# All eight experts add into the output, VectorE's order in the relation stage is written out, and loads and copies around it move

## The chip, the cores and the metric

The kernel runs on one core of one Trainium2 chip. The metric is device time in microseconds (us) of one execution, as the median of several; lower is better. The engines are TensorE (PE), VectorE (DVE), ScalarE (ACT), GpSimd (POOL) and SyncE (SP). SP and POOL start most of the DMAs here, ACT a few.

## The reference

Four residual layers on 625 tokens of 1024 numbers, each on the layernorm of `x` (cut to what matters):

```python
# 1 relational graph convolution with a gate (8 relations; edges: src, dst, edge_type)
out = x @ root + bias
for r in range(8):
    sums = segment_sum(x[src] * (edge_type == r), dst)
    cnt = segment_sum(edge_type == r, dst)
    out = out + (sums / max(cnt, 1)) @ weight[r]
z = concat([u, x]) @ w_gate + b_gate          # u is out
h = tanh(u) * z + x * (1 - z)
# 2 int8 feed-forward:  x_int8 @ weight_int8.T, scaled, plus bias
# 3 graph convolution:  segment_sum(norm * (x @ W.T + b)[col], row)
# 4 mixture of 8 experts, top 2, capacity 196 slots per expert
logits = x @ router_w
combine, dispatch = top2_gating(logits, capacity)
expert_in = einsum('nec,nh->ech', dispatch, x)
hmid = silu(einsum('ech,ehf->ecf', expert_in, w1) + b1)
expert_out = einsum('ecf,efh->ech', hmid, w2) + b2
y = einsum('nec,ech->nh', combine, expert_out)
out = y + 0.1 * (silu(x @ sw1 + sb1) @ sw2 + sb2)     # and x + out
```

## The kernel before

Tokens lie in five tiles (`t`) of 125 partitions (P = 125, NT = 5); the 1024 columns are worked in two halves (`h`, HC = 512).

*Products of weights.* Nine products of the normalized tokens with a 1024 x 1024 weight (relations 0 to 6, the gate's x half, relation 7) run on PE by a scheme with seven block products in place of eight (L431, combinations on VectorE). Relations 0 to 6 go to DRAM as `yd`; the rows of relation 7, the last product, stay in SBUF. Meanwhile VectorE and GpSimd count, for each relation, the edges from each token to each token, into the DRAM table `counts`.

*The relation stage* (L571 to L707) goes through the relations in the order 7, 0, 1, ... 6 (`order`; `n` is the place in it). For each relation, half and tile, `products` (L629) multiplies counts with rows `y`: five source tiles, each in two parts, so ten matmuls into one PSUM tile. The two parts are `hi`, a rounded copy that ScalarE makes (L602), and `lo`, the rest, which VectorE gets by subtraction (L606, the split). VectorE then does `X += ps * rc` (L684). `rc` is one over the number of edges: VectorE adds the counts over the five source tiles (`over_sources`, L614 and L616), PE sums them (`number`, L642), VectorE inverts (L648, L649). `over_relations` sums the counts over relations into `btot`, by ScalarE's copy for the first relation (L622) and VectorE's additions for the others (L624). While half 0 of a relation is multiplied, its half 1 is split and the next relation's `over` is summed; during half 1 the next relation's half 0 is split and `btot` is summed. In each tile's step the code writes L684, a split, and a count addition; a planner decides the order in which VectorE executes them from their due times, within the bounds that data and `behind` set.

*Orders.* `behind(a, b)` only says that `a` is issued after `b` on an engine; `after` makes it wait for the end of `b`. `in_order` chains SP's loads in the order of the code: the count tiles (`load_counts`, three buffers `bp`), rows (`load_y`) and weights (`weight_block`). `on_pe` and `in_steps` chain PE's work.

*The gate stage* (L710 to L828) multiplies by `w_gate`, whose four 1 MB blocks `gate_w` are loaded at n = 5. Its normalized tiles `th` are transposed between the gate's tiles, `th[t - 2]` at t = 2 and 3.

*The experts.* The router's masks (L1063 to L1147) give each token its slot in two experts. `fill_slots` (L1159) makes, by small matmuls, for each expert's 196 slots (two groups of 98, index `j`) the token number `token_i` and the gate's weight; an empty slot's token number points to a spare row past the 625. `find_others` and `fill_others` (L1187, L1198) find tokens that are not in an expert, one for each empty slot, so that an empty slot can add zero to some row of `out`: `out_i`. Before the change this is made for experts 4 to 7 (NL = 4) only: VectorE makes 20 one-hot tiles `spots`, PE sums them with 40 matmuls.

`shared_out` (L1227) finishes the tokens' base value in `X` (VectorE's `z` and `X` additions) and stores it. Then, for each expert e, come the gather of its tokens (L1278, GpSimd), transposes, two matmul steps (L1294, L1322), the scaling (L1329, VectorE, into `ye`, two buffers in the memory of `aT` and `btot`) and the addition of the rows to DRAM (L1339, GpSimd's indirect DMA that adds; two per expert, four half as wide for expert 7, with `half_i`). Each addition waits for those of the expert before, because two experts may add to one row.

The base goes into a DRAM tensor `total`, which has spare rows for empty slots. Experts 0 to 3 add to `total` at `token_i`; one copy `out <- total` (L1363, on SP) follows once they have landed; experts 4 to 7 wait for it and add to `out` at `out_i`.

A second, exact version of everything stands under a condition on the counts that does not hold for these inputs.

Of the kernel before, what the change touches and what calls it, by code (L numbers as in the profile page):

```python
# [35 lines left out]
NL = 4  # L36
# [11 lines left out]
def layers(  # L48
# [166 lines left out]
    total = dram.tile([N + 2 * CP, D], F32, name="total")  # L215
# [358 lines left out]
    bp = convs.enter_context(tc.tile_pool(name="bp", bufs=3))  # L574
    hp = convs.enter_context(tc.tile_pool(name="hp", bufs=2 * NT))
    crp = convs.enter_context(tc.tile_pool(name="crp", bufs=2))
# [4 lines left out]
    counted, over, parts = {}, {}, {}  # L581

    def load_counts(r):
        counted[r] = bp.tile([P, NT, N], FR, tag="b", name="b")
        for d in spread(nc.sync, counted[r].bitcast(F32), counts[r].rearrange("(k p) d -> p k d", p=P)):
            after(in_order(d), group)

    def load_y(r, h):
        for k in range(NT):
            y = yp.tile([P, HC], FR, tag="y", name="y")  # L590
            for d in spread(nc.sync, y.bitcast(F32), ydram[r][:, h, k, :]):
                in_order(d)
            held.setdefault(r, {})[k, h] = y

    def split(r, h, k):

        y = held[r][k, h].bitcast(F32)
        if exact:
            parts[r, h, k] = [y]
            return  # L600
        hi = hp.tile([P, HC], F32R, tag="hi", name="hi")
        nc.scalar.copy(hi, y)  # L602
        lo = held[r][k, h]
        if r == order[0]:
            lo = yp.tile([P, HC], F32R, tag="y", name="y")
        nc.vector.tensor_sub(lo, y, hi.bitcast(F32))  # L606
        parts[r, h, k] = [lo, hi]

    def over_sources(r, k):

        v = counted[r].bitcast(F32)
        if k == 1:
            over[r] = crp.tile([P, N], FR, tag="over", name="over")
            d = nc.vector.tensor_add(over[r], v[:, 0, :], v[:, 1, :])  # L614
        else:
            d = nc.vector.tensor_add(over[r], over[r].bitcast(F32), v[:, k, :])  # L616
        behind(d, posted[-1])

    def over_relations(r, k):
        v = counted[r].bitcast(F32)[:, k, :]  # L620
        if r == order[0]:
            behind(nc.scalar.copy(btot[:, k, :], v), copied[-1])  # L622
        else:
            behind(nc.vector.tensor_add(btot[:, k, :], btot[:, k, :], v), posted[-1])  # L624
# [41 lines left out]
    for k in firsts:  # L666
        split(order[0], 0, k)
    for n, r in enumerate(order):
        if n == R - 3:
            gate_w = [[weight_block(w_gate, i, h) for i in range(2)] for h in range(2)]  # L670
        for h in range(2):
            hs = slice(h * HC, (h + 1) * HC)
            for t in range(NT):
                ps = mm_tile()
                on_pe(products, ps, r, h, t, firsts if n == 0 and h == 0 else range(NT))
                if (n, h, t) == (0, 0, 0):
                    on_pe(number, r)
                if h == 1 and t == 0 and n + 1 < R:
                    on_pe(number, order[n + 1])
                if n == R - 1 and h == 1:  # L680
                    on_pe(turn_u, t, 0)
                    if t > 0:
                        on_pe(turn_u, t - 1, 1)
                nc.vector.scalar_tensor_tensor(  # L684
                    X[t][:, hs],
                    ps[:P, :],
                    rc[:, r, t : t + 1],
                    X[t][:, hs],
                    op0=ALU.mult,
                    op1=ALU.add,  # L690
                )
                if h == 0:
                    split(r, 1, t)
                    if t > 0 and n + 1 < R:
                        over_sources(order[n + 1], t)
                else:
                    if n + 1 < R:
                        split(order[n + 1], 0, t)
                    over_relations(r, t)
            if n == 0 and h == 0:  # L700
                load_y(order[1], 0)
                load_y(order[1], 1)
            elif 0 < n + h and n + 1 + h < R:
                load_y(order[n + 1 + h], 1 - h)
        if n + 3 < R:
            load_counts(order[n + 3])
# [68 lines left out]
    for t in range(NT):  # L775
# [4 lines left out]
        for h in range(2):  # L780
            with tc.issue_after(pe_last.ins):
                pe_last, added = gate(t, h)
            if h == 0 and t >= 2 and t < NT - 1:
                on_pe(transposed, xT, (t - 2) * P, th[t - 2], P)
            if t > 0:
                nc.scalar.copy(wb[(t - 1) // 2][:, (t - 1) % 2 * 2 + h, :], w8[:, 2 * (t - 1) + h, :])
# [159 lines left out]
    cleared = []  # L946
    for v in (tokens, total):
        for j in range(2):
            cleared.append(nc.scalar.dma_start(v[N + j * CP : N + (j + 1) * CP, :], zrow))
# [124 lines left out]
    NM = 2 * NE + NL  # L1074
# [19 lines left out]
    nc.vector.tensor_add(others, masks[:, :, 0, NE - NL :], masks[:, :, 1, NE - NL :])  # L1094
# [80 lines left out]
    spots = aT_flat[:, : NL * NT * CAP // 2].bitcast(BF16)  # L1175
    spots = spots.rearrange("p (e t c) -> p e t c", e=NL, t=NT)
    before = mp.tile([P, NT, NL], F32, name="before")
    out_i = mp.tile([CP, 2, NL], I32, name="out_i")
    half_i = mp.tile([CP, 2, 2], I32, name="half_i")

    def find_others():

        nc.vector.tensor_scalar(before, others, -float(N), float(N), op0=ALU.mult, op1=ALU.add)
        nc.vector.tensor_add(before, before, pos_all[:, :NT, 2 * NE :])
        for e in range(NL):
            for t in range(NT):
                d = nc.vector.tensor_scalar(  # L1187
                    spots[:, e, t, :], io_cap, before[:, t, e : e + 1], None, op0=ALU.is_equal
                )
                behind(d, numbered[-1])  # L1190

    def fill_others(_):
        ps = ps_sm.tile([128, HC], F32, tag="sm", name="others")
        ps = ps[:CP, : 4 * NL].rearrange("p (j e v) -> p j e v", j=2, e=NL)
        for j in range(2):
            for e in range(NL):
                for t in range(NT):
                    last = nc.tensor.matmul(  # L1198
                        ps[:, j, e, :],
                        spots[:, e, t, j * CP : (j + 1) * CP],  # L1200
                        digits[:, t, :],
                        start=(t == 0),
                        stop=(t == NT - 1),
                    )
        rest_of = mp.tile([CP, 2, NL], F32, name="rest_of")
        taken_of = slots[:, :, NE - NL :, 0]
        nc.vector.tensor_scalar(rest_of, ps[:, :, :, 0], float(P), None, op0=ALU.mult)
        nc.vector.tensor_add(rest_of, rest_of, ps[:, :, :, 1])
        nc.vector.tensor_scalar(out_i, taken_of, -1.0, 1.0, op0=ALU.mult, op1=ALU.add)
        nc.vector.tensor_mul(rest_of, rest_of, out_i)  # L1210
        nc.vector.tensor_add(out_i, rest_of, slots[:, :, NE - NL :, 1])
        for h in range(2):
            nc.vector.tensor_scalar(
                half_i[:, h, :], out_i[:, :, NL - 1], 2.0, float(h), op0=ALU.mult, op1=ALU.add
            )
        return last
# [3 lines left out]
    base = []  # L1220

    def shared_out(t):
# [16 lines left out]
        base.extend(spread(nc.sync, total[t * P : (t + 1) * P, :], X[t]))  # L1239
# [3 lines left out]
    find_others()  # L1243
    in_steps(((shared_out, 0), (shared_out, 1), (fill_others, None), *((shared_out, t) for t in range(2, NT))))
# [8 lines left out]
    def rows_at(j, e, direct=False):  # L1253
        at = out_i[:, j, e - NE + NL :][:, :1] if direct else token_i[:, j, e : e + 1]
        return bass.IndirectOffsetOnAxis(ap=at, axis=0)

    def flat_rows(v):
        return v[:N, :].rearrange("n d -> (n d)").rearrange("(a b) -> a b", a=80)
# [17 lines left out]
    def gather(e):  # L1276
        for j in range(2):
            nc.gpsimd.indirect_dma_start(  # L1278
                out=rows_of_slots(e, j), out_offset=None, in_=tokens, in_offset=rows_at(j, e)
            )  # L1280
# [25 lines left out]
    done = sent  # L1306
    sent = base + cleared

    def expert_out(e):
# [4 lines left out]
        for j in range(2):  # L1314
# [3 lines left out]
            for h in range(2):  # L1318
# [15 lines left out]
                if e < NE - 1:  # L1334
                    to, at, v = total if e < NE - NL else out, rows_at(j, e, e >= NE - NL), ye[:, j, :]
# [18 lines left out]
    for e in range(NE):  # L1354
# [5 lines left out]
        if e == NE - NL:  # L1360
            for n in range(e + 4, NE):
                load_weights(n)
            d = in_order(nc.sync.dma_start(flat_rows(out), flat_rows(total)))  # L1363
            after(d, [*sent, *done])
            sent = [d]
# [62 lines left out]
```

## Time and profile before

| | us |
|---|---|
| three runs | 1248.88, 1250.09, 1253.97 (median 1250.09) |
| the profiled execution | 1246.61 |
| its span, first to last recorded instruction | 1244.9 |
| PE busy (share of the span) | 1188.5 (95%) |
| VectorE busy | 837.9 (67%) |
| GpSimd busy | 487.0 (39%) |
| ScalarE busy | 172.2 (14%) |
| mean clock granted to TensorE | 0.985 |
| L629, 800 matmuls of the relation stage | 323.5 |
| L606, 80 splits, mean of one | 53.0 relation stage, 0.680 each |
| PE's last matmul (L1322) starts | 1221.69, for 0.59 |

A row of the timeline has the start, the length, the engine, the source line, the operation, output and inputs, and in brackets the idle time before it and what ended that. Equal instructions that follow one another are put together (x5). A row of the windows has the stretch, its length and each engine's busy time and instructions, then the clock granted to TensorE (1.00 is full), the busy share of the DMA engines and GB/s. A row of the waits has what waited, for what, the sum, how often, and the longest.

### The profile page before, as it was taken

How to read it: one execution, taken by the hardware profiler on the slowest of the kernel's cores; microseconds unless marked ns; L12 is line 12 of the kernel's file. 1: busy time of each engine (PE TensorE's matmuls, PEld its weight loads, DVE VectorE, ACT ScalarE, POOL GpSimd, SP SyncE). 2: the span in 40 equal slices, each digit the busy share in tenths (PEclk: the TensorE clock that was granted, in tenths of full speed). 3: DMA queues.
4: the chain of work that ended last, by engine and by line, in shares of the span. 5: the costliest groups of instructions: out<-in, count | busy, mean ns of one | idle time of the engine just before them, and what ended most of it. 6: DMA issues, size and time to landing. Idle time of an engine off the chain costs nothing. (4 is left out here: it accounts for less than half of the span.)

```text
span 1244.9 us, 11083 instructions
## 1 busy us (share of the span) xinstructions
PE 1188.5 (95%) x3810; PEld 649.8 (52%) x3810; DVE 837.9 (67%) x1340; ACT 172.2 (14%) x308; POOL 487.0 (39%) x227
## 2 busy tenths in 40 slices
PE   5999999999999999999999999899999999999992
PEld 2444444444444444444448887685445447756661
DVE  6879888888888888865149778755979416452210
ACT  1100000000000000000022122113321111313330
POOL 1005787888787888888500000004210000043312
PEclk9999999999999999999989999999999999999996
DMA  9995737373636364535455667606430025279964
GB/s 263 267 255 131 200 65 198 66 198 70 194 75 188 81 183 87 146 78 142 76 142 156 168 161 198 216 1 167 118 136 16 17 84 177 79 223 279 278 186 71
DMA packets 156288, 181.72 MB, mean 146 GB/s; under 512 B 78513, under 2 KB 95272, under 8 KB 156160
## 3 DMA queue, kind: packets, MB, share of 16 engines
q1 hardware_dynamic: 66162, 134.84, 36.7%
q0 software_dynamic: 72992, 13.31, 10.5%
q10 hardware_dynamic: 17070, 32.78, 8.6%
q8 instruction: 32, 0.52, 0.2%
q14 instruction: 32, 0.26, 0.1%
HBM read 134.22 MB, written 48.86 MB: 147 GB/s over the span
## 5 line engine op out<-in xcount | busy, mean ns | idle before, releaser
L389 POOL DMA_INDIRECT table<-hits,idx x165 | 403.8, 2447 | 199.4 <-DMA kr<-key_rows 99.7
L431 PE MATMUL mm<-w,xT 128*125 128x512 f32 x800 | 350.9, 593 | 0.0
L365 DVE SCALAR_TENSOR_TENSOR junk<-kr,key,wm 125x1375 f32<-125x1375 f32 x165 | 271.4, 1645 | 1.1
L431 PEld LDWEIGHTS mm<-w,xT 128*125 128x125 f32 x800 | 150.2, 188 | 191.7 <-issue 189.1
L629 PE MATMUL mm<-y,b 125*125 125x512 f32 x400 | 163.0, 407 | 9.1 <-DVE y L606 6.7
L629 PE MATMUL mm<-hi,b 125*125 125x512 f32 x400 | 160.5, 401 | 0.0
L431 PE MATMUL mm<-t,btot 128*125 128x512 f32 x320 | 143.8, 592 | 0.0
L1278 POOL DMA_INDIRECT th<-tokens,token_i x16 | 21.5, 1345 | 205.0 <-DVE aT L1187 172.7
L431 PEld LDWEIGHTS mm<-t,btot 128*125 128x125 f32 x320 | 60.1, 188 | 77.3 <-issue 77.3
L684 DVE SCALAR_TENSOR_TENSOR X<-mm,rc,X 125x512 f32<-125x512 f32 x80 | 59.9, 749 | 51.5 <-PE mm L629 50.4
L952 POOL IOTA io<- 125x40 f32 x1 | 0.2, 208 | 239.3 <-PE mm L629 239.3
L629 PEld LDWEIGHTS mm<-y,b 125*125 125x125 f32 x400 | 75.9, 190 | 32.2 <-DVE y L606 11.1
L629 PEld LDWEIGHTS mm<-hi,b 125*125 125x125 f32 x400 | 76.1, 190 | 18.1
L900 PE MATMUL mm<-w,xT 128*125 128x512 f32 x160 | 70.0, 595 | 2.4 <-ACT xT L187 2.4
L431 PE MATMUL mm<-w,btot 128*125 128x512 f32 x160 | 71.9, 592 | 0.0
L431 PE MATMUL mm<-t,xT 128*125 128x512 f32 x160 | 71.9, 592 | 0.0
L746 PE MATMUL mm<-w,xT 128*125 128x512 f32 x160 | 69.3, 592 | 0.0
L602 ACT CAST hi<-y 125x512 fp32r<-125x512 f32 x80 | 43.3, 617 | 147.2 <-PE mm L629 132.4
L1322 PE MATMUL mm<-w,th 128*98 128x512 f32 x128 | 56.3, 592 | 0.0
L606 DVE TENSOR_TENSOR y<-y,hi 125x512 fp32r<-125x512 f32 x80 | 53.0, 680 | 0.7 <-ACT hi L602 0.7
L450 ACT COPY y<-mm 125x512 f32<-125x512 f32 x18 | 10.5, 586 | 302.0 <-PE mm L431 291.7
L900 PEld LDWEIGHTS mm<-w,xT 128*125 128x125 f32 x160 | 29.6, 188 | 39.7 <-issue 36.0
(219 smaller groups left out, 1165.4 us busy)
## 6 DMA issues: line engine op xcount, KB each, us to landing
w<-in_L_gnn_weight_dram SPq DMA_DIRECT2D x32, 1024.0 KB
w<-in_L_ffn_w_dram SPq DMA_DIRECT2D x16, 1024.0 KB
yd<-y ACTq DMA_DIRECT2D x70, 224.0 KB
y<-yd SPq DMA_DIRECT2D x70, 224.0 KB
table<-zero SPq DMA_DIRECT2D x4, 3054.0 KB
b<-table SPq DMA_DIRECT2D x8, 1367.2 KB
kr<-key_rows ACTq DMA_DIRECT2D x15, 601.6 KB
w<-in_L_gnn_w_gate_dram SPq DMA_DIRECT2D x8, 1024.0 KB
```

The source lines that it names most:

```text
L365: d = nc.vector.scalar_tensor_tensor(junk, kr, key[:, c : c + 1], wm[:, (EG - 1 - j) * P : (2 * EG - 1 - j) * P], op0=ALU.is_equal, op1=AL ...
L389: d = nc.gpsimd.indirect_dma_start(out=table, out_offset=bass.IndirectOffsetOnAxis(ap=idx[:, c : c + 1], axis=0), in_=hits[:, c : c + 1], ...
L431: last = nc.tensor.matmul(ps[:P, :], lhs[:, k], rhs[:, k], start=(start and k == 0), stop=(stop and k == 3))
L450: nc.scalar.copy(put(NT - 1, h), ps[:P, :])
L602: nc.scalar.copy(hi, y)
L606: nc.vector.tensor_sub(lo, y, hi.bitcast(F32))
L629: last = nc.tensor.matmul(ps[:P, :], counted[r][:, k, t * P : (t + 1) * P], part, start=(k == ks[0] and part is parts[r, h, k][0]), stop=( ...
L684: nc.vector.scalar_tensor_tensor(X[t][:, hs], ps[:P, :], rc[:, r, t : t + 1], X[t][:, hs], op0=ALU.mult, op1=ALU.add,)
L746: last = nc.tensor.matmul(ps[:P, :], xT[:, 4 * i + k, t * P : (t + 1) * P], gate_w[h][i][:, k, :], start=(i == 0 and k == 0), stop=(i == 1 ...
L900: last = nc.tensor.matmul(ps[:P, :], xT[:, k, t * P : (t + 1) * P], gcn_w[h][k // 4][:, k % 4, :], start=(k == 0), stop=(k == KD - 1),)
L1278: nc.gpsimd.indirect_dma_start(out=rows_of_slots(e, j), out_offset=None, in_=tokens, in_offset=rows_at(j, e))
L1322: last = nc.tensor.matmul(ps[:CP, :], he[:, f, j * CP : (j + 1) * CP], weights[e][1][:, f, hs], start=(f == 0), stop=(f == 1),)
```

## The change

- `NL` and `total` go. `tokens` alone is cleared in its spare rows; the base is stored to `out`; the copy L1363 goes; all eight experts add into `out` at `out_i`.
- The masks of "others" cover eight experts: 40 one-hots in place of 20, ten after each of the first four `shared_out`, and 80 matmuls in `fill_others`, which comes after the fifth `shared_out` instead of the second.
- In the relation stage `in_turns` and `turns` chain VectorE's accumulations, splits and count additions in one order. In half 0: accumulation 0, splits 0 and 1; accumulation 1, split 2, `over` 1; accumulation 2, split 3, `over` 2; and so on. In half 1 likewise, with `btot` 0 to 4. The first half is special: its first accumulation comes after tile 1, with three splits there.
- The first relation's `over` additions go behind `posted[-3]` in place of `posted[-1]` (`posted` lists VectorE's additions of the weight products); the first split is issued ahead of them. `number` of that relation follows tile 1 in place of tile 0.
- ScalarE's `hi` copies go behind its last copy in the units (`copied[-1]`), and the `btot` copies behind the last upper half's copy.
- Count tiles have named memory `b0`, `b1`, `b2`; the third lies in memory of its own pool `bp2`. The first rows of the second relation have tiles of their own (`yp2`) and are loaded before the loop.
- The four blocks of `w_gate` are loaded one per half at n = 3 and 4, in place of all four at n = 5.
- In the gate stage `th[t - 3]` is transposed at t = 3 and 4.

```diff
-    total = dram.tile([N + 2 * CP, D], F32, name="total")
...
-    bp = convs.enter_context(tc.tile_pool(name="bp", bufs=3))
+    bp = convs.enter_context(tc.tile_pool(name="bp", bufs=1))
+    bp0, bp1 = (bp.tile([P, NT, N], FR, tag=f"b{i}", name=f"b{i}") for i in range(2))
     hp = convs.enter_context(tc.tile_pool(name="hp", bufs=2 * NT))
+    bp2 = convs.enter_context(tc.tile_pool(name="bp2", bufs=1))
+    yp2 = convs.enter_context(tc.tile_pool(name="yp2", bufs=NT))
...
-        nc.scalar.copy(hi, y)
+        upper.append(nc.scalar.copy(hi, y))
+        behind(upper[-1], copied[-1])
...
-        nc.vector.tensor_sub(lo, y, hi.bitcast(F32))
+        turns.append(nc.vector.tensor_sub(lo, y, hi.bitcast(F32)))
+        if len(turns) > NT:
+            behind(*turns[:-3:-1])
...
+    def in_turns(d):
+        if turns:
+            behind(d, turns[-1])
+        turns.append(d)
...
-        behind(d, posted[-1])
+        if r == order[0]:
+            behind(d, posted[-3])
+        else:
+            in_turns(d)
...
-            behind(nc.scalar.copy(btot[:, k, :], v), copied[-1])
+            d = nc.scalar.copy(btot[:, k, :], v)
+            if not exact:
+                behind(d, upper[2 * NT - 1])
         else:
-            behind(nc.vector.tensor_add(btot[:, k, :], btot[:, k, :], v), posted[-1])
+            in_turns(nc.vector.tensor_add(btot[:, k, :], btot[:, k, :], v))
...
+    load_y(order[1], 0)
+    gate_w = [[], []]
     for n, r in enumerate(order):
-        if n == R - 3:
-            gate_w = [[weight_block(w_gate, i, h) for i in range(2)] for h in range(2)]
         for h in range(2):
+            if n in (3, 4):
+                gate_w[n - 3].append(weight_block(w_gate, h, n - 3))
...
-                if (n, h, t) == (0, 0, 0):
+                if (n, h, t) == (0, 0, 1):
                     on_pe(number, r)
...
+                for k in ((0, 1), (2,), (3,), (4,), ())[t] if n + h > 0 else ((), (0, 1, 2), (3,), (4,), ())[t]:
+                    if h == 0:
+                        split(r, 1, k)
+                    elif n + 1 < R:
+                        split(order[n + 1], 0, k)
+                for k in ((), (1,), (2,), (3,), (4,))[t] if h == 0 else ((), (0,), (1,), (2,), (3, 4))[t]:
+                    if h == 1:
+                        over_relations(r, k)
+                    elif n + 1 < R:
+                        over_sources(order[n + 1], k)
...
-            if h == 0 and t >= 2 and t < NT - 1:
-                on_pe(transposed, xT, (t - 2) * P, th[t - 2], P)
+            if h == 0 and t >= 3:
+                on_pe(transposed, xT, (t - 3) * P, th[t - 3], P)
...
-    NM = 2 * NE + NL
+    NM = 3 * NE
...
-        base.extend(spread(nc.sync, total[t * P : (t + 1) * P, :], X[t]))
+        for d in spread(nc.sync, out[t * P : (t + 1) * P, :], X[t]):
+            after(d, done)
+            base.append(d)
...
-    find_others()
-    in_steps(((shared_out, 0), (shared_out, 1), (fill_others, None), *((shared_out, t) for t in range(2, NT))))
+    for t in range(NT):
+        in_steps(((shared_out, t),))
+        for e in range(2 * t, min(2 * t + 2, NE)):
+            find_others(e)
+    in_steps(((fill_others, None),))
...
-                    to, at, v = total if e < NE - NL else out, rows_at(j, e, e >= NE - NL), ye[:, j, :]
+                    to, at, v = out, rows_at(j, e, out_i), ye[:, j, :]
...
-        if e == NE - NL:
-            for n in range(e + 4, NE):
-                load_weights(n)
-            d = in_order(nc.sync.dma_start(flat_rows(out), flat_rows(total)))
-            after(d, [*sent, *done])
-            sent = [d]
```

## The prediction

> **What bounds the kernel now.** I read the shares of busy time first, then the waits of TensorE (PE), then the timeline around the longest of them, then windows for the granted clock, then the timeline of GpSimd (POOL) at the end.
>
> ```profile
> PE 1188.5 (95%) x3810; PEld 649.8 (52%) x3810; DVE 837.9 (67%) x1340; ACT 172.2 (14%) x308; POOL 487.0 (39%) x227
> PE tr L184 <- DVE X L169: 10.1, 1, 10.1
> PE mm L629 <- DVE y L606: 6.7, 4, 4.3
> ```
>
> PE works 1188.5 of 1244.9 us, so a change pays only where PE waits, where its clock falls, or after its last matmul. The first wait, 10.1 us, is the layernorm at the start, which nothing here touches. The second lies in the relation stage; this is its longest piece:
>
> ```profile
> 804.88 0.80 DVE L616 TENSOR_TENSOR over<-over,b 125x625 fp32r<-125x625 f32 x1
> 805.60 2.24 DVE L624 TENSOR_TENSOR btot<-btot,b 125x625 f32<-125x625 f32 x3
> 807.76 3.09 DVE L606 TENSOR_TENSOR y<-y,hi 125x512 fp32r<-125x512 f32 x5
> 808.49 0.50 PE L629 MATMUL mm<-y,b 125*125 125x512 f32 x1 [4.32 <-DVE y L606]
> 808.00:810.00 2.00, 1.51 (x4) 1.09 (x5) 2.00 (x4) 0.00 (x0) 0.00 (x0) 0.72 0.00 0
> 810.00:812.00 2.00, 2.00 (x6) 1.50 (x6) 0.84 (x2) 0.00 (x0) 0.00 (x0) 0.50 0.00 0
> ```
>
> VectorE (DVE) did four count additions (L616, L624) while PE stood idle for the split of the first row (L606). In the two windows the next-to-last three columns are clock, DMA share and GB/s: the clock then fell to 0.50. So a stall costs twice. The whole price comes from the spacing of the accumulations (L684), one per tile: 8.49 us across this stall where a full-speed tile takes 2.32, so 6.17 lost; from 773.24 to 787.92, with the stalls of 1.25 and 0.59, 14.68 against 4 x 2.32 + 2.88 = 12.16, so 2.52 lost. From 654.38 to 822.54 all of them take 168.16 against 67 x 2.32 + 7 x 0.5 = 158.9: no other loss there exceeds 0.6.
>
> PE's last matmul ends at 1222.29, and 22.6 us follow in which only additions into the output land:
>
> ```profile
> 1180.69 3.23 SPq L1363 DMA_DIRECT2D out_dram<-total  x1
> 1199.63 1.55 POOL L1339 DMA_INDIRECT out_dram<-aT,out_i  x1 [23.13 <-SPq L1384]
> 1211.42 1.52 POOL L1339 DMA_INDIRECT out_dram<-btot,out_i  x1 [0.30 <-issue]
> 1218.86 1.53 POOL L1339 DMA_INDIRECT out_dram<-aT,out_i  x1 [5.92 <-DMA out_dram<-btot,out_i]
> 1220.69 1.52 POOL L1339 DMA_INDIRECT out_dram<-aT,out_i  x1 [0.30 <-issue]
> 1229.24 1.53 POOL L1339 DMA_INDIRECT out_dram<-btot,half_i  x1 [7.03 <-DMA out_dram<-aT,out_i]
> 1234.72 1.52 POOL L1339 DMA_INDIRECT out_dram<-btot,half_i  x1 [0.30 <-issue]
> ```
>
> The 2.5 MB copy holds expert 4's additions until 1199.63, though VectorE had its rows at 1182.75. Experts 5 to 7 queue behind, each pair waiting for the pair before to land (1211.42 to 1218.86 is 7.44, 1220.69 to 1229.24 is 8.55).
>
> **The change, part by part.** *The end.* Without the copy, expert 4's pair starts near 1181 and expert 5's near 1195; both have landed when expert 6 needs them. Expert 6's second half-rows: VectorE's last two L1329 would fall at 1208.5 and 1210.1 as now (PE itself had no wait there). GpSimd sometimes waited for the third L1329 (expert 3: start 1167.46, third one done 1167.02), so the pair starts 1209.6 and 1211.4. It lands at 1218.9 to 1220.0 by the two durations above. Expert 7's four follow every 1.83: last start 1218.9 + 0.2 + 5.5 = 1224.6 (VectorE's last rows, 1223.08, are no bound). From the last start to the end the trace has 1244.9 - 1234.72 = 10.18. End 1234.8 to 1235.9: gain 9.0 to 10.1; I take 9.9, nearer the pair that ran with as little beside it. Upper bound of a landing: expert 0 to 1, 1126.75 to 1138.56, 11.8 while weights load; then the gain is 5.7. Lower: none faster than 7.44 is seen.
>
> An estimate stands apart here: the Trainium skill ("DMA: Bandwidth & Descriptors", "Anatomy of one DMA — SWDGE (gpsimd) path") gives 2.0 us plus bytes over 436 GB/s for GpSimd's DMA, so 2.9 us for 401 KB; by it expert 7's last addition would follow its rows (1223.08 + 0.3) and the end come at 1233.6. The measured 7.44 decides.
>
> *More one-hots and `others` matmuls.* L1187 makes 40 instead of 20, ten behind each of four `shared_out`; 20 x 0.235 = 4.7 us more of VectorE, spread under the 19.4 us that the 40 matmuls of L1227 take. The last one-hot ends about 1110.0 and PE's last `shared_out` about 1107.3; the order on PE is now five `shared_out`, then L1198, then expert 0's transposes. L1198 had 40 matmuls in 1.96 us, so 80 take 3.92: +1.96, and about 0.1 at the join, +2.1. If VectorE's order let the last tile's one-hots come later, PE would wait up to 10 x 0.235 = 2.4. The clock: L1159's small matmuls were followed by this,
>
> ```profile
> 1088.00:1089.00 1.00, 1.00 (x7) 0.76 (x7) 0.54 (x5) 0.47 (x2) 0.00 (x0) 0.88 1.05 371
> 1090.00:1091.00 1.00, 1.00 (x2) 0.34 (x1) 1.00 (x5) 0.00 (x0) 1.00 (x1) 0.50 1.03 416
> 1092.00:1093.00 1.00, 1.00 (x3) 0.38 (x2) 1.00 (x6) 0.00 (x0) 1.00 (x1) 0.91 0.27 94
> ```
>
> so 3.57 us of tiny matmuls cost 0.12 + 3 x 0.5 + 0.09 = 1.7, while the 1.96 us of L1198 were followed by 1.00 throughout. 3.92 us of L1198 and then 1.8 us of transposes resemble the first: I take +1.6, bounds 0 and 3.4 (twice as long a drop).
>
> The skill speaks against this edit: "TensorE: Matmul & The Clock Gate" ("Part 1: The HAM clock gate", "Part 4: PE-mode transpose") says that an idle-looking window of about 3.4 us throttles the array and that transposes do not count as activity. The drop after L1159 agrees. By the rule alone a second drop is near sure, and the sum below stands; by L1198's own row it would be 1.6 lower.
>
> The base goes straight into `out` in the same six stores; two queue behind a weight load on SP's queue, and expert 0's pair waits for them: it started at 1123.31 behind a weight load already, and could be some 3 us later (two issues of 1.3 each, as the six take 7.62) with 14.06 us of PE per expert to recover in, so 0. `b2` of expert 7 waits for the later L1198, is needed at 1211 and hides under six experts. `tokens` alone is cleared: two fewer stores, off the path.
>
> *Fixed VectorE order.* In each later half the first two splits come right behind the first accumulation and the count additions behind the splits. Work is the same: per half five accumulations at 0.67 apart (804.21 to 804.88), five splits at 0.62 (3.09 for five) and four or five additions at 0.72 (2.16 for three): 9.3 to 10.1, against 11.6 of PE. So the 6.17 and 2.52 go: -8.7. Bounds: 0 if the slack of 1.5 us is spent elsewhere, -9.2 by the full sum. The copies of the upper halves (L602) go behind ScalarE's last copy: five take 2.70 a half and ScalarE is busy 14%, so 0; late next would be the split behind each.
>
> *The start.* VectorE's first act at 639.21 is an `over` (0.72 back to back) ahead of the split that L629 needs:
>
> ```profile
> 639.21 0.80 DVE L614 TENSOR_TENSOR over<-b 125x625 fp32r<-125x625 f32 x1
> 639.93 0.68 DVE L606 TENSOR_TENSOR y<-y,hi 125x512 fp32r<-125x512 f32 x1
> 640.71 0.47 PE L629 MATMUL mm<-y,b 125*125 125x512 f32 x1 [2.15 <-issue]
> 642.00:646.00 4.00, 3.79 (x7) 2.11 (x8) 4.00 (x7) 0.00 (x0) 0.00 (x0) 0.50 0.64 185
> ```
>
> That addition now stands behind. PE begins up to 0.7 earlier; -0.5, bounds +0.8 (the first accumulation now comes a tile later and holds a bank) and -3.7, the half-speed stretch 642 to 651.8 shortened if PE starts without the gap. `number` moves one tile, same work. Relation two's rows have own tiles and load from about 636 instead of 640.64, behind the third count load, which now waits for a unit buffer; needed after 654, hidden unless more than 10 us late. One transposition in the gate stage moves a tile later: no PE wait stood there and the count is equal, 0; late next would be FFN operands, bound 0.6.
>
> *w_gate.* Its four 1 MB loads leave the place where they stood together (766 to 773) and go one by one into the halves of the fourth and fifth relation (n = 3, 4), behind each half's rows on SP: 2 x 1.28 MB of rows, 1.5 of counts and 2 of gate per 23.7 us, some 250 GB/s. Windows 770 to 790 moved 300 and 323 GB/s. Rows are asked for a half ahead, so 0; the slow rival prices the other case.
>
> Sum: -9.9 + 2.1 + 1.6 - 8.7 - 0.5 = -15.4. Profiled 1246.61 (span 1244.9 and 1.7 around it) becomes 1231.2; the median of 1250.09 lies 3.5 above the profiled one, so 1234.7.
>
> **Rivals.** (a) *The relation stalls only move.* For: slack is 1.5 us a half, and a split needs ScalarE's copy, then VectorE. Against: both stalls stood behind count additions, never behind copies. The -8.7 falls away: 1243.4. (b) *The end gains little.* If pairs into `out` land in 11.8, the end gains 5.7 instead of 9.9: 1238.9; if something else holds the last pair as long, 1244.6. For: eight experts now add where four did, and the first ran at 11.8. Against: nothing loads after 1185. (c) *Slower: the gate's loads starve the rows.* If the rate while they load falls under 250 GB/s so that rows come over half a relation late, each of four halves stalls like 808 did: 4 x 6.17 = +24.7, 1234.7 + 24.7 = 1259.4. For: DMA share was 1.05 when they loaded before. Against: 300 GB/s was reached then. (d) *The clock never drops at the start:* -3.7 for -0.5, 1231.5.
>
> **Chances.** Forecast 0.68, (a) 0.11, (b) 0.08, (c) 0.05, (d) 0.08. Half a per cent, 6.25 us, is what a measurement can tell: faster 0.92, same 0.04, slower 0.04 (c with little of it). Range: 1228, where (d) meets the best landing and no second drop, to 1243, where (a) ends.
>
> **What would show it.** Right: no L629 wait over 0.5 us between 654 and 822, accumulations of that stretch within 160 us; expert 4's pair within 4 us of its rows; last matmul to end about 12 to 13 us instead of 22.6; half-clock windows behind the `others`. Wrong: a wait on `y` by DMA at n = 3 or 4, or GpSimd still waiting over 5 us ahead of expert 6.

## The result and the profile after

The changed kernel takes 1231.49 us (median of four, 1228.55 to 1232.26) against 1250.05 of the kernel before: a ratio of 0.9842, 95% interval 0.9815 to 0.9869. The forecast was 1234.7, the range 1228 to 1243. Its profiled execution took 1231.8 with a span of 1230.0, 14.9 less than the span before.

The page of the kernel after, its first part, and the rows of PE's waits that answer to those shown before:

```profile
PE 1192.4 (97%) x3850; PEld 653.6 (53%) x3850; DVE 846.7 (69%) x1360; ACT 172.2 (14%) x308; POOL 487.2 (40%) x227
```

```profile
PE tr L183 <- DVE X L168: 10.0, 1, 10.0
...
PE mm L649 <- issue: 1.4, 1, 1.4
...
PE mm L649 <- DVE y L614: 0.6, 1, 0.6
```

The 6.7 us of waits for a split have shrunk to one of 0.6 at the start of the relation stage (L629 is L649 now, the split L614, the accumulation L712). PE is 4 us busier: it has 40 more small matmuls (1.9 us) and more time at half clock. Where the time went, by PE's milestones in the two profiled executions:

| milestone | before | after | difference | change since the line above |
|---|---|---|---|---|
| end of the weight products | 638.57 | 638.54 | 0.0 | |
| last accumulation of the relation stage starts | 848.71 | 838.60 | -10.1 | -10.1 |
| last gate matmul starts | 922.16 | 913.75 | -8.4 | +1.7 |
| last int8 matmul starts | 981.55 | 974.65 | -6.9 | +1.5 |
| last `slots` matmul starts | 1088.18 | 1081.19 | -7.0 | -0.1 |
| first expert's first matmul starts | 1111.3 | 1106.2 | -5.1 | +1.9 |
| last matmul starts | 1221.7 | 1217.8 | -3.9 | +1.2 |
| end | 1244.9 | 1230.0 | -14.9 | -11.0 |

In the relation stage VectorE now works like this (timeline of the kernel after, VectorE, same place as the stall shown before):

```profile
802.54 0.75 DVE L712 SCALAR_TENSOR_TENSOR X<-mm,rc,X 125x512 f32<-125x512 f32 x1 [0.83 <-PE mm L649]
803.21 0.15 DVE L668 TENSOR_SCALAR reached<-tr 125x5 f32<-125x5 f32 x1
803.28 0.68 DVE L614 TENSOR_TENSOR y<-y,hi 125x512 fp32r<-125x512 f32 x1
...
805.43 0.75 DVE L712 SCALAR_TENSOR_TENSOR X<-mm,rc,X 125x512 f32<-125x512 f32 x1 [0.69 <-PE mm L649]
806.10 0.68 DVE L614 TENSOR_TENSOR y<-y,hi 125x512 fp32r<-125x512 f32 x1
806.69 0.81 DVE L644 TENSOR_TENSOR btot<-btot,b 125x625 f32<-125x625 f32 x1
807.75 0.75 DVE L712 SCALAR_TENSOR_TENSOR X<-mm,rc,X 125x512 f32<-125x512 f32 x1 [0.25 <-PE mm L649]
```

Each accumulation is followed by a split and only then by one count addition, and VectorE waits for PE, no longer PE for VectorE. At the end, GpSimd's additions of the kernel after (start, length, operation, idle time before and what ended it):

```profile
1176.48 1.55 POOL L1374 DMA_INDIRECT out_dram<-aT,out_i  x1 [3.87 <-DMA out_dram<-btot,out_i]
1179.16 1.54 POOL L1374 DMA_INDIRECT out_dram<-aT,out_i  x1 [1.14 <-DVE aT L1364]
1189.79 1.52 POOL L1374 DMA_INDIRECT out_dram<-btot,out_i  x1 [9.08 <-DVE btot L1364]
1193.22 1.52 POOL L1374 DMA_INDIRECT out_dram<-btot,out_i  x1 [1.91 <-DVE btot L1364]
1203.85 1.52 POOL L1374 DMA_INDIRECT out_dram<-aT,out_i  x1 [9.11 <-DVE aT L1364]
1207.28 1.52 POOL L1374 DMA_INDIRECT out_dram<-aT,out_i  x1 [1.91 <-DVE aT L1364]
1214.33 1.52 POOL L1374 DMA_INDIRECT out_dram<-btot,half_i  x1 [5.54 <-DVE btot L1364]
...
1219.81 1.52 POOL L1374 DMA_INDIRECT out_dram<-btot,half_i  x1 [0.30 <-issue]
```

From expert 5 on no addition waits for another to land: they wait for their own rows from VectorE, and the last three follow the one before. The last one starts 10.15 before the end, as it did before (10.16), but 1.4 after PE's last matmul ends instead of 12.4. What is new is half clock in other places (windows of the kernel after; the column before the last two is the granted clock):

```profile
842.00:846.00 4.00, 4.00 (x8) 1.67 (x7) 0.00 (x0) 4.00 (x5) 0.37 (x2) 0.57 0.98 256
921.00:928.00 7.00, 6.30 (x24) 4.88 (x25) 5.66 (x15) 2.64 (x6) 0.00 (x0) 0.51 0.01 2
1081.00:1085.00 4.00, 4.00 (x11) 1.89 (x10) 1.95 (x12) 1.30 (x2) 2.09 (x2) 0.57 1.05 394
1105.00:1109.00 4.00, 4.00 (x17) 3.77 (x18) 1.07 (x7) 1.29 (x3) 1.97 (x2) 0.57 1.01 308
```

The third had its like before (1088 to 1093) and the fourth was forecast. The first two are where the table's +1.7 and +1.5 arise; the second lies among transpositions with waits, so that 3.41 by the clock cost PE only 1.5.

### The profile page after: what moved, and what is told of

The parts are those of the page before. It is cut to its first block, busy times and chain, and to the rows that moved or that the text cites. A ratio compares the mean times of both kernels' runs of the same rounds, so it can differ in the third digit from the quotient of the medians.

```text
span 1230.0 us, 11161 instructions
## 1 busy us (share of the span) xinstructions
PE 1192.4 (97%) x3850; PEld 653.6 (53%) x3850; DVE 846.7 (69%) x1360; ACT 172.2 (14%) x308; POOL 487.2 (40%) x227
## 4 chain that ended last, share of the span: by engine, by line
PE 91%; DMA 4%; ACT 2%; DVE 1%; issue 1%; POOL 0%; SPq 0%; ACTq 0%; POOLq 0%; DVEq 0%
PE mm L429 48%; PE mm L649 14%; PE mm L777 6%; PE mm L931 6%; PE mm L1357 4%; PE mm L1330 3%; PE mm L959 2%; DMA w<-in_L_gnn_weight_dram 2%; PE tr L183 2%; PE mm L1259 2%; PE mm L908 1%; PE mm L1045 1%; DMA y<-yd 1%; PE lgT L1032 1%; ACT xT L186 1%
## 5 line engine op out<-in xcount | busy, mean ns | idle before, releaser
L387 POOL DMA_INDIRECT table<-hits,idx x165 | 408.1, 2474 | 198.7 <-DVE idx L383 99.3
L429 PEld LDWEIGHTS mm<-w,xT 128*125 128x125 f32 x800 | 150.1, 188 | 192.3 <-issue 188.6
L649 PE MATMUL mm<-y,b 125*125 125x512 f32 x400 | 160.7, 402 | 2.3 <-issue 1.4
L649 PE MATMUL mm<-hi,b 125*125 125x512 f32 x400 | 159.1, 398 | 0.0
L1314 POOL DMA_INDIRECT th<-tokens,token_i x16 | 17.4, 1086 | 214.5 <-DVE token_i L1198 174.4
L649 PEld LDWEIGHTS mm<-y,b 125*125 125x125 f32 x400 | 75.0, 187 | 23.6 <-DVE y L614 3.4
L712 DVE SCALAR_TENSOR_TENSOR X<-mm,rc,X 125x512 f32<-125x512 f32 x80 | 60.0, 751 | 38.8 <-PE mm L649 38.0
L649 PEld LDWEIGHTS mm<-hi,b 125*125 125x125 f32 x400 | 75.1, 188 | 18.2
L614 DVE TENSOR_TENSOR y<-y,hi 125x512 fp32r<-125x512 f32 x80 | 53.6, 681 | 0.0
L422 DVE TENSOR_TENSOR t<-w,t 128x2048 f32<-128x2048 f32 x20 | 45.8, 2290 | 8.1 <-DMA w<-in_L_gnn_weight_dram 7.6
```

The lines of the kernel that those rows point to most:

```text
L387: d = nc.gpsimd.indirect_dma_start(out=table, out_offset=bass.IndirectOffsetOnAxis(ap=idx[:, c : c + 1], axis=0), in_=hits[:, c : c + 1], ...
L422: d = nc.vector.tensor_sub(o, v, w)
L429: last = nc.tensor.matmul(ps[:P, :], lhs[:, k], rhs[:, k], start=(start and k == 0), stop=(stop and k == 3))
L614: turns.append(nc.vector.tensor_sub(lo, y, hi.bitcast(F32)))
L649: last = nc.tensor.matmul(ps[:P, :], counted[r][:, k, t * P : (t + 1) * P], part, start=(k == ks[0] and part is parts[r, h, k][0]), stop=( ...
L712: nc.vector.scalar_tensor_tensor(X[at][:, hs], v[:P, :], rc[:, r, at : at + 1], X[at][:, hs], op0=ALU.mult, op1=ALU.add,)
```

## The experiments

Each ratio is to the kernel before on the same chip. The "loss" or "worth" of a half-clock stretch is the sum of (1 - clock) over windows of 1 us.

**1. The end alone, and the relation stage alone.** `tail_only` is the kernel before with the diff's parts on `total`, `out`, the masks and the others; `rel_only` has the parts on the relation stage, the loads and the gate stage. The diffs are those of the change.

> The kernel before with the change's end alone (base into out, no copy, eight experts into out, 40 one-hots and 80 matmuls); relation stage as before. My account: from PE's last matmul to the end 11 to 12 us in place of 22.6 (-11.0), the others +1.9, a half-clock stretch of about 3 us behind them +1.3 to 1.6: together -7.6, some 1242.5 against 1250. Rival, that the copy was hidden and something else held the last pair: the end stays near 22 us and the time rises by 3, to 1253.

> The kernel before with the change's relation stage, load order and gate-stage transposition alone; the end as before. My account: the accumulations of the stage end 10.1 us earlier (1.3 at the start, 8.85 from the two stalls), and the copy still holds the end: 1240, within 3.4 for half-clock stretches in the gate stage and before the int8 layer, which the trace of after has and that of before lacks. If those two stretches come from the change itself they appear here too (842 and 921) and the gain is 6.7; if they come by chance, not always. Rival, that the parts need each other: less than 5 gained.

Measured: `tail_only` 1242.04, ratio 0.9946 (0.9922 to 0.9969); `rel_only` 1238.94, ratio 0.9914 (0.9884 to 0.9944). The product of the two is 0.9861, the whole change 0.9842: the parts add up and do not need each other. In `tail_only` PE keeps its 6.7 us of waits on `y`, and the end shrinks to 11.9 us. The stretches at 842 and 920 stand in the profile of `rel_only` and not in that of `tail_only`, as they would if this part of the change brought them; the last section shows what goes with the first of them instead.

**2. VectorE's order.** `no_chain` leaves the planner to order VectorE, with everything else of the change in place:

```diff
-        turns.append(nc.vector.tensor_sub(lo, y, hi.bitcast(F32)))
-        if len(turns) > NT:
-            behind(*turns[:-3:-1])
+        nc.vector.tensor_sub(lo, y, hi.bitcast(F32))
...
     def in_turns(d):
-        if turns:
-            behind(d, turns[-1])
-        turns.append(d)
+        behind(d, posted[-1])
```

> After without the chain of VectorE's accumulations, splits and count additions (the code's order of writing, the copies, tiles and loads stay; the planner orders VectorE). If the written-out order is what removes the stalls: PE waits on y in the later relations come back, one of 3 us or more, and 4 to 9 us of the time. Rival, that the copies or the earlier splits in the code suffice: no wait over 0.5 us, the time of after.

Measured: 1248.31, ratio 0.9988 (0.997 to 1.0006): all that the change gains is gone, 17 us over the kernel after where 4 to 9 were expected. Its profile has two places with stalls. VectorE and PE at the second (timeline of `no_chain`; L613 is the split, L707 the accumulation, L624, L626 and L639 count additions):

```profile
807.51 0.80 DVE L624 TENSOR_TENSOR over<-b 125x625 fp32r<-125x625 f32 x1
808.23 0.80 DVE L639 TENSOR_TENSOR btot<-btot,b 125x625 f32<-125x625 f32 x1
808.95 0.80 DVE L626 TENSOR_TENSOR over<-over,b 125x625 fp32r<-125x625 f32 x1
809.67 0.74 DVE L707 SCALAR_TENSOR_TENSOR X<-mm,rc,X 125x512 f32<-125x512 f32 x1
810.33 0.68 DVE L613 TENSOR_TENSOR y<-y,hi 125x512 fp32r<-125x512 f32 x1
```

```profile
811.07 0.50 PE L644 MATMUL mm<-y,b 125*125 125x512 f32 x1 [1.94 <-DVE y L613]
...
812.39 0.50 PE L644 MATMUL mm<-y,b 125*125 125x512 f32 x1 [0.59 <-DVE y L613]
...
813.71 0.50 PE L644 MATMUL mm<-y,b 125*125 125x512 f32 x1 [0.59 <-DVE y L613]
...
815.75 0.79 PE L644 MATMUL mm<-y,b 125*125 125x512 f32 x1 [1.28 <-DVE y L613]
```

Three count additions stand ahead of the splits; in the kernel before there were four. The waits named there and at 778 to 782 are 7.0 us in seven pieces, one of them (1.03 at 781.91) for rows from DRAM; each place also has a half-clock stretch that costs 5.1. Together that is 17.2 of the 17.6 by which the stage (weight products' end to last accumulation) is longer than in the profile of after: 217.6 against 200.05.

`written_order` keeps the chain, but in the order of the code before:

```diff
-                for k in ((0, 1), (2,), (3,), (4,), ())[t] if n + h > 0 else ((), (0, 1, 2), (3,), (4,), ())[t]:
+                for k in ((0,), (1,), (2,), (3,), (4,))[t] if n + h > 0 else ((), (0, 1), (2,), (3,), (4,))[t]:
...
-                for k in ((), (1,), (2,), (3,), (4,))[t] if h == 0 else ((), (0,), (1,), (2,), (3, 4))[t]:
+                for k in ((), (1,), (2,), (3,), (4,))[t] if h == 0 else ((0,), (1,), (2,), (3,), (4,))[t]:
```

> After with the chain of VectorE kept, but in the order in which the code of before writes it: in each tile's step one accumulation, one split, one count addition (no split ahead). If a fixed order is all that is needed: the last split of a half ends 1.5 us after the last accumulation and is needed 1.9 us after it, so no wait over 0.5 us and the time of after (within 2 us). If the two splits ahead are needed: a wait on y at the start of each half, up to 0.5 us in 15 halves and half-clock stretches with them, 3 to 10 us longer than after.

Measured: 1231.45, ratio 0.9865 (0.9831 to 0.9898), no wait on `y` over 0.6, the stage 200.9 long. That VectorE's order is fixed is the gain; that two splits go ahead is not needed. Both runs keep the change's copies, tiles and loads; the chain without these was not tried.

**3. The place of w_gate's loads.** `gate_late` loads the four blocks at n = 5 again.

```diff
+        if n == R - 3:
+            gate_w = [[weight_block(w_gate, i, h) for i in range(2)] for h in range(2)]
         for h in range(2):
-            if n in (3, 4):
-                gate_w[n - 3].append(weight_block(w_gate, h, n - 3))
```

> After with w_gate's four blocks loaded together at n = 5 again. If VectorE's order alone was behind the stalls near 781 of before: no wait on y there, same time as after (1231.5 within 2). Rival, that those two stalls (2.5 us) came from rows that arrived late behind the four blocks: the waits near 777 to 782 are back and the time is 2 to 3 us longer.

Measured: 1230.89, ratio 0.9848 (0.9817 to 0.9879), no wait near 781. The place of these loads costs and gains nothing that shows; the two stalls near 781 of before were VectorE's order as well.

**4. The copy two experts earlier.** `nl6` is the kernel before with `NL = 6`: experts 0 and 1 add into `total`, then comes the copy, and six experts add into `out`.

```diff
-NL = 4
+NL = 6
...
-            for n in range(e + 4, NE):
-                load_weights(n)
             d = in_order(nc.sync.dma_start(flat_rows(out), flat_rows(total)))
```

> The kernel before with the copy two experts earlier: experts 0 and 1 add into the other tensor, then the copy, then experts 2 to 7 add into out (30 one-hots and 60 matmuls). If only the copy's place held the end: the queue of additions catches up (14.06 of PE an expert against 7.4 to 12 for a landing), the end is 11 to 12 us after PE's last matmul, the time 1250 - 11 + 1 (20 more matmuls) and up to 1.7 for a half-clock stretch: 1240 to 1242, as tail_only. Rival, that additions into out by eight (or six) experts land slower than those of four: pairs still wait for each other at experts 6 and 7, end 15 us or more after PE, 1244 or more.

Measured: 1244.2, ratio 0.9972 (0.9959 to 0.9985): a miss, the end gains half of what was expected. GpSimd's additions in the profile of `nl6`, with the copy:

```profile
1156.71 1.32 SPq L1361 DMA_DIRECT2D out_dram<-total  x1
...
1174.40 1.55 POOL L1339 DMA_INDIRECT out_dram<-aT,out_i  x1 [22.69 <-DMA out_dram<-total]
...
1187.98 1.55 POOL L1339 DMA_INDIRECT out_dram<-btot,out_i  x1 [7.60 <-DVE aT L1329]
...
1197.99 1.55 POOL L1339 DMA_INDIRECT out_dram<-aT,out_i  x1 [4.01 <-DMA out_dram<-btot,out_i]
...
1207.80 1.52 POOL L1339 DMA_INDIRECT out_dram<-btot,out_i  x1 [6.42 <-DMA out_dram<-aT,out_i]
...
1216.95 1.52 POOL L1339 DMA_INDIRECT out_dram<-aT,out_i  x1 [5.81 <-DMA out_dram<-btot,out_i]
```

The copy takes 17.7 us from issue to the first addition behind it, and leaves expert 2 some 20 late (first additions of experts 0 and 2 lie 28.2 apart in the kernel after, 1126.66 + 28.2 = 1154.9). From there first addition follows first addition by 13.6 to 9.2, and PE needs 14.06 an expert: a few us are won back with each, and a stretch worth 3.4 behind its 60 small matmuls takes the rest of the gain in time. After the five experts that follow expert 2 the end still lies 17.2 behind PE's last matmul, against 22.6 in the kernel before, where three follow expert 4, and 11.6 without a copy. So it is the copy's wait of some 20 us that counts. The additions of six experts into `out` land no slower than those of four: where a pair waited for the pair before, it began 8.2, 8.0 and 7.3 us after that pair's last start, in the kernel before 8.1, 7.4 and 8.5. The rival's sign (pairs still waiting at 6 and 7) was there, for another reason than the rival gave.

**5. The half-clock stretches.** `spread` makes the 80 small matmuls in four pieces, `fillers` puts spare matmuls where PE waits at the start of the relation stage, `old_start` undoes two edits of the start:

```diff
# spread: in the loop over t, behind find_others, and behind expert 0's expert_hidden
+        if t > 1:
+            in_steps(((fill_others, 2 * t - 4),))
...
-    in_steps(((fill_others, None),))
...
+        if e == 0:
+            in_steps(((fill_others, NE - 2),))
...
# fillers: in products, first tile of the stage
+            for i in range(0 if spare is None else 6 if k == ks[0] else 2):
+                d = nc.tensor.matmul(
+                    spare[:P, :], counted[r][:, 0, :P], parts[r, 0, 0][1], start=True, stop=True
+                )
...
# old_start
-            behind(d, posted[-3])
+            behind(d, posted[-1])
...
-                if (n, h, t) == (0, 0, 1):
+                if (n, h, t) == (0, 0, 0):
```

> After with the 80 small matmuls of the others in four pieces: 20 each after the third, fourth and fifth shared_out, and the last 20 after the first expert's first matmuls. If 3.9 us of tiny matmuls and the transposes behind them cause the half-clock stretch at 1105: it goes, 1.7 us less than after (1229.8). Rival, that it comes by chance of where the stretch lies: half-clock stretches appear there or at the slots at about the same rate, and the time is that of after.

> After with 14 matmuls into a spare PSUM tile where PE waits at the start of the relation stage (6 ahead of the first product, 2 ahead of each of the next four). If PE's idle time there causes the half-clock stretch of 641 to 648: it goes, the accumulations come 3 us earlier and the time is 2 to 3.4 us less than after (1228 to 1229.5). Rival, that the drop has another cause (the matmuls of these shapes, or the change of work): the stretch stays and the time is that of after or up to 1 us longer.

> After with the start of the relation stage as before: over ahead of the first split, number behind tile 0. If the start's 1.3 us come from there: first product 0.7 later, a half-clock stretch worth 5.1 in place of 3.4 or less, the accumulations 1 to 2.5 us later than in after and the time 1 to 2.5 longer. Rival, that the gain was the chance length of the stretch: 0.7 or nothing.

Measured: `spread` 1228.51, ratio 0.9853 (0.9824 to 0.9881); `fillers` 1228.0, ratio 0.9844 (0.9818 to 0.987); `old_start` 1230.93, ratio 0.985 (0.9811 to 0.9888). None of these times alone can be told from the kernel after. The profiles can. With `fillers` the start reads (PE, then windows; L651 is the spare matmul, L658 the product):

```profile
637.78 1.96 PE L651 MATMUL spare<-hi,b 125*125 125x512 f32 x6
639.72 0.49 PE L658 MATMUL mm<-y,b 125*125 125x512 f32 x1
640.06 0.39 PE L658 MATMUL mm<-hi,b 125*125 125x512 f32 x1
640.29 0.63 PE L651 MATMUL spare<-hi,b 125*125 125x512 f32 x2
641.05 0.50 PE L658 MATMUL mm<-y,b 125*125 125x512 f32 x1
```

```profile
638.00:642.00 4.00, 3.87 (x15) 2.26 (x13) 3.62 (x6) 3.70 (x8) 0.00 (x0) 1.00 1.10 275
642.00:646.00 4.00, 3.63 (x14) 2.18 (x13) 2.96 (x5) 1.85 (x4) 0.00 (x0) 1.00 1.02 195
```

The clock stays at 1.00 where the kernels before and after have 0.50, and the stage from the products' end to the last accumulation takes 198.8, against 199.8 to 201.0 in the profiles of after, its repeat and `rel_only`. The two versions of experiment 6 with these spare matmuls show the same (1.00 and 198.8), and all eleven profiles without them have a drop there. So the clock falls because PE waits there, once for 1.4 us and up to four times for 0.6 or less. The gain is 1.0 to 2.2 us, not the 3 that was expected, and `fillers` has three stretches of 3.41 elsewhere (917, 1077 and 1101).

`old_start` was to bring back the old start, and did not. VectorE and PE in the kernel after and in `old_start`:

```profile
639.19 0.68 DVE L614 TENSOR_TENSOR y<-y,hi 125x512 fp32r<-125x512 f32 x1
639.79 0.81 DVE L629 TENSOR_TENSOR over<-b 125x625 fp32r<-125x625 f32 x1
639.97 0.47 PE L649 MATMUL mm<-y,b 125*125 125x512 f32 x1 [1.43 <-issue]
```

```profile
638.73 0.68 DVE L614 TENSOR_TENSOR y<-y,hi 125x512 fp32r<-125x512 f32 x1
639.32 0.80 DVE L629 TENSOR_TENSOR over<-b 125x625 fp32r<-125x625 f32 x1
639.50 0.47 PE L649 MATMUL mm<-y,b 125*125 125x512 f32 x1 [1.43 <-issue]
```

In both the split goes ahead of the `over` addition, and PE's first wait is 1.43; in the kernel before the addition (639.21) stood ahead of the split (639.93) and the wait was 2.15. So `old_start` says nothing against that order as the cause of the earlier product; it only shows that the two edits that it undoes are not what set the order. Its stage is 201.9 long, with a stretch worth 5.12; one profile does not settle whether that length is its own.

The others: in the eight profiles with 80 small matmuls in one piece (after, its repeat, `tail_only`, `gate_late`, `no_chain`, `written_order`, `fillers`, `old_start`) a half-clock stretch begins within 2 us of their end each time, a loss of 1.71 or 3.41; behind 60 in one piece (`nl6`) it does too, behind 40 (before and `rel_only`) it does not, and in the three with the pieces it never does.

**6. The kernel after again, and two versions that go further,** on one chip. `best` is `spread` and `fillers` together with eight more spare matmuls ahead of the last `turn_u` (PE's transpositions for the gate stage), where PE waits 2.09; `best2` adds two small ones ahead of each group of transpositions at 915 to 926:

```diff
+    if not exact:
+        on_pe(busy, order[-1])
     on_pe(turn_u, NT - 1, 1)
...
+                if j0 == 0:
+                    nc.tensor.matmul(spare_q[:P, :P], ident[:P, :P], ones, start=True, stop=True)
+                    nc.tensor.matmul(spare_q[:P, :P], ident[:P, :P], ones, start=True, stop=True)
```

> The changed kernel itself, beside the runs below on one chip, since chips differ by some us: 18 to 19 us less than before. If half-clock stretches come by chance, the profile has another set of them than the first one (which had 641, 842, 921, 1081, 1105), each worth a multiple of 1.71.

> After with the others spread, the 14 spare matmuls at the start of the relation stage and 8 more where PE waits 2.09 for ScalarE's last copies of the stage. No half-clock stretch at 641 nor 842, none at 1105: 3 to 5 us less than after (the start 2 to 3.4, the others up to 1.7, 842 sometimes 1.7). Rival, that stretches spared there come elsewhere: less than 1.5 gained.

> As the run before it, with two spare matmuls of ident and ones (125 columns, float32) ahead of each of the five groups of transpositions of 915 to 926, where PE waits 0.56 for ScalarE each time. If those waits and transpositions give the stretch of 6.8 us at half clock: it never shows there and the median falls by 0.5 to 1.5. Rival, that the spare matmuls cost what they fill: 0 to 1 us longer.

Measured: the kernel after 1231.59 (1230.87 to 1233.74), ratio 0.987 (0.9833 to 0.9907); `best` 1226.21 (1225.18 to 1229.62), ratio 0.9829 (0.9797 to 0.9862); `best2` 1225.15 (1224.17 to 1227.96), ratio 0.9811 (0.978 to 0.9842). No execution of `best` or `best2` is slower than the fastest of after on that chip. Of the profile of `best`, the places where after had half clock:

```profile
842.00:846.00 4.00, 4.00 (x11) 1.82 (x10) 0.00 (x0) 4.00 (x5) 0.00 (x0) 1.00 0.95 238
921.00:928.00 7.00, 7.00 (x38) 4.61 (x37) 6.79 (x13) 1.06 (x2) 0.00 (x0) 1.00 0.00 0
1099.00:1103.00 4.00, 3.57 (x28) 3.18 (x26) 1.76 (x3) 1.75 (x4) 2.76 (x2) 1.00 0.91 289
```

Only one stretch is left in it before PE's last matmul (1076, worth 1.71). Whether `best2`'s last edit adds to `best` is open: 1 us lies within both ranges, and the stretch at 921 was missing in `best`'s profile too.

## Why the prediction was right, point by point

- *The two stalls, -8.7.* Right, measured -8.84: from accumulation 6 to 68, counted from 0, the kernel before takes 156.01 us and after 147.17. `no_chain` and `written_order` show that the order is the cause.
- *The start, -0.5.* Right in sign; the term was mis-sized, -1.3 in the profiles. The first product comes 0.74 earlier as forecast, with the split ahead of the `over` addition as the prediction had it. Beside that a stretch worth 3.41 stands in place of 5.12; its length varies between profiles (1.71 to 5.12 with the changed stage), so the part beyond 0.7 is partly luck. Which of the edits puts the split ahead was not found: with the two that `old_start` undoes gone, it still goes ahead.
- *The end, -9.9.* Right, measured -11.0. The step mis-sized was expert 6: I let it wait for the third L1329 and let expert 7 wait for its landing. Its first addition went 0.3 behind the second L1329, which makes the last of its rows (1203.55 to 1203.85). The row that I read for the third, expert 3's 1167.46 in the kernel before, came 2.2 after its rows and 12.3 after the last start of expert 2's pair, so by these times it was rather a landing that it waited for. Expert 7's first addition began 7.05 behind the one before and still waited for rows, so a landing there takes less than the 7.44 that I took for the fastest. The end is PE's last matmul, a last addition 1.4 later, and 10.15.
- *The others, +2.1 and +1.6.* +1.9 measured, then a stretch worth 1.71 (+1.2 in the table). The Trainium skill's rule on transposes and idle windows ("TensorE: Matmul & The Clock Gate", "Part 1: The HAM clock gate" and "Part 4: PE-mode transpose") was the better guide to the outcome than the row of L1198: eight profiles of eight have the drop behind 80, and with pieces of 20 none of three. That transposes do not count is not borne out by every row: in the kernel before PE did nothing but transpositions from 924.93 to 931.75, busy for 0.62 of it, and the clock stayed at 1.00.
- *The loads, the tiles, the transposition, the base: 0.* `gate_late` confirms it for w_gate; the others were not tried alone. The slow rival, rows late behind the gate's loads, did not appear in the profiles with the new place, but for one wait of 1.03 us for rows in `no_chain` (781.91), well after these loads.
- *Not in the sum:* +3.2 of half-clock stretches in the gate stage and ahead of the int8 layer in the profiled execution. With them the profiled gain is 14.8, near the 15.4 forecast though the end and the start gave more than forecast: that the two nearly cancel is luck. The medians moved by 18.6, since the profiled execution of before (1246.61) was quicker than all four timed ones and that of after a middling one; on another chip the medians moved by 16.4. The forecast added 3.5 for a median above the profiled time; the kernel after's median lies 0.3 below, and that is nearly all of the 3.2 by which 1234.7 was too high.

Rival (a), stalls that only move, is refuted for the fixed order; rival (b), an end that gains little, by the 11.6 us that are left behind PE's last matmul; rival (d), the clock that does not drop at the start, needed the spare matmuls.

## What to carry to other kernels

When an engine at 70% makes PE wait, look at what stands ahead of the awaited instruction in its queue before looking at its load: here the written-out order was worth nine us, and the same code without it lost 17.6 in this stage. Merging through a second tensor and a copy puts the copy's whole latency into a chain of dependent additions, which here won back only a few us a step. Tiny matmuls in pieces of 20 kept PE's clock where 80 in one piece did not, and where PE must wait a microsecond or two, spare matmuls can keep it: `best` was 5.4 us quicker than the kernel after on the same chip.

## What the runs showed of the hardware

Each half-clock stretch ahead of PE's last matmul, in all fourteen profiles, costs a multiple of 1.71 by the granted clock: 1.71, 3.41 or 5.12, that is 3.4, 6.8 or 10.2 us at half clock. The Trainium skill ("TensorE: Matmul & The Clock Gate", "Part 1: The HAM clock gate") has a free-running window of 3413 ns; these lengths agree with it.

The starts agree too. Within each profile they lie whole multiples of 3.413 us apart: in the kernel after they are at 641.09, 842.48, 920.98, 1081.41 and 1105.30, which is 59, 23, 47 and 7 steps. Where this grid lies differs from one execution to the next, and so the same wait can be followed by a drop or not. The kernel before has the wait of 2.09 at the end of the relation stage as well. Cut into such windows, the least busy one around this wait has PE busy for 1.32 of 3.41 us in the profile of after, and the clock falls at its end; the repeat has 2.10 and the kernel before 1.64, and no drop. Of the twelve profiles without spare matmuls there, the five with a drop have 0.39 to 0.43 of the window busy, the seven without one 0.46 to 0.63. So the stretch at 842 goes with the place of the grid. Whether the change makes such places likelier is not shown: the three profiles with the old relation stage have the grid in nearly the same place there.

So which stretches an execution gets is partly chance: the same kernel had 842, 921, 1081 and 1105 in one profile and 923, 1080 and 1104 in another. Executions of the kernel before run from 1245.57 at a mean clock of 0.985 to 1255.97 at 0.975 on one chip, so much of the spread of the times goes with these stretches.

In the tail of the kernel before, the next expert's additions began 7.4 to 8.5 us after the last start of the pair before where they waited for its landing, and all fourteen profiles have 10.1 to 10.8 from the last start to the end. The estimate of 2.9 us from the Trainium skill ("DMA: Bandwidth & Descriptors", "Anatomy of one DMA — SWDGE (gpsimd) path") is far too short for an addition that GpSimd starts.
